# Two pieces of a spectral stage moved into the rounds of the attention before it

## The chip, the core and the metric

The kernel runs on one core of a Trainium2 chip. A core has five engines that each take their own instructions in order: PE (TensorE, matrix products, with its weight loads counted apart as PEld), DVE (VectorE), ACT (ScalarE), POOL (GpSimd) and SP (SyncE, which here only issues DMAs). They meet through semaphores. Operands lie in SBUF (128 partitions), matrix results in PSUM (eight banks of 128 x 512 float32), and the large arrays in HBM. Times are device microseconds (us) of one execution.

## The reference, cut to what is touched

Two layers of a "metaformer" on eight images of 128 channels and 32 x 32 = 1024 tokens. Only the first layer matters here: an attention, and then a spectral unit whose first step is a forward sine and cosine sum over the tokens of each image.

```python
# layer 0
x = x + _L0_conv_ref(_ln_c(x), wq, wk, wv)       # attention, 8 heads of 16
t = _to_tokens(x)
t = t + _L0_ffn_ref(_ln_t(t), sigma, phi, M_u, M_plus, M_minus, ...)
x = _from_tokens(t, x)
...
def _ln_t(v, eps=1e-5):                           # over the channels of a token
    m = jnp.mean(v, axis=-1, keepdims=True)
    s = jnp.var(v, axis=-1, keepdims=True)
    return (v - m) / jnp.sqrt(s + eps)
...
Vf   = jnp.fft.rfft(phi, n=n, axis=0)             # filters
Uf_p = jnp.fft.rfft(u, n=n, axis=1)               # forward sums of an image
```

## The kernel before, in words

**The attention** (`attention_bounded`) is one long list of steps sorted by hand. `at(round, order, step)` puts a step into a round; the list is sorted by round, then by order, and every engine gets its instructions in that sequence. There are 256 rounds, 32 to an image (`first = 32 * b`), four to a unit (a quarter of the queries and half of the heads). If `t0` is the first round of a unit, then:

- `scores` (round `t0 + r`, order 0): 16 matmuls on PE into the only bank group `s`, then the exponential on ACT into a tile `e` (L598, L603).
- `add_tiles` (order 1): POOL adds the two halves of `e` into `t` (L612).
- `sums` and `reciprocals` (round `t0 + 5`, orders 4 and 5): PE adds `t` into `z` (L619), DVE takes the reciprocal `r` (L626).
- `spread_out` (round `t0 + 6`, order 2.5): PE spreads `r` into `rb` (L633).
- `divide` (rounds `t0 + 6` to `t0 + 9`, order 3): DVE multiplies `e` by `rb` (L640).
- `values` (rounds `t0 + 8` to `t0 + 11`): PE multiplies with the values into `av` (L650).
- `take` and `results` (rounds `t0 + 11`, `t0 + 12` of every second unit): ACT takes `av` out, PE turns it, ACT copies it to `at`, POOL adds it to the tokens `xt` (L660 to L674). These are the rounds 0 modulo 8. After the last quarter SP writes the image to HBM as `x1d` (L676).

Rounds 0 modulo 4 thus hold the third `divide` of a unit, and rounds 1 modulo 4 the fourth `divide` and after it the reciprocal of the next unit.

Between these lie the preparation of the next image: `load`, two `tokens` (turn the image, copy to `xt`), the 25 pieces of a layer norm (`layer_norm_pieces`: eight pairs of statistics on DVE, L79 and L80; nine pieces with 17 small POOL instructions, L87 to L99; eight normalisations on ACT, L105), two `channels`, and eight projections `keys`, `queries`, `key_values`. All these small PE results, `z` too, use one PSUM bank ("z"), so that each waits until the one before is taken out.

For image 0 the norm is made ahead (`BoundedAttention.tokens`), but its tokens are turned a second time in round 0 to have `xt`. Image 1 has its turns in rounds 8 and 12 and its norm in rounds 9 to 19.

**The spectral stage** (`Spectral.forward`) is in program order on every engine. It loads images 1, 2 and 3 (`Head.load`, L1650), makes eight sine tables `t` (`table`: on DVE two instructions with L1711 and one with L1712, on ACT one sine, L1713), norms images 1 and 2, and then takes the images in turn: `image` (PE sums p_half, L1882; ACT copies `other`, L1888; DVE adds and subtracts into `us`, L1895; PE turns), then the norm of image b + 3, then `parts`. Of image 0 the load and the norm are already made within the attention's last rounds (`Head.pieces`, one piece a round, from L745).

Of the kernel before, what the change touches and what calls it, by code (L numbers as in the profile page):

```python
# [18 lines left out]
P = 128  # L19
# [380 lines left out]
class BoundedAttention:  # L400
# [6 lines left out]
    def __init__(self, nc, cp):  # L407
        self.nc = nc
        HG, NH = self.HG, self.NH
        self.xc = cp.tile([P, T], F32, name="xc")  # L410
        self.ht = cp.tile([P, NT, C], F32, name="ht")
        self.hk = [cp.tile([P, T], F32, name=f"hk{n}") for n in range(2)]
        self.wq = cp.tile([P, HG, NH, 32], F32, name="wq")
        self.wk = cp.tile([C, C], F32, name="wk")
        self.wv = cp.tile([C, HG, NH, HD], F32, name="wv")
        self.group = cp.tile([P, NG], F32, name="group")
        self.spread = cp.tile([P, 2, P], F32, name="spread")
# [4 lines left out]
    def tokens(self, x, ident, pool, ps):  # L422

        nc = self.nc
        nc.sync.dma_start(self.xc, x[0].rearrange("c h w -> c (h w)"))
        xv = self.xc.rearrange("c (i p two) -> c two i p", two=2, p=P)
        st = pool.tile([P, NT, 6], F32, name="f_st")
        mv = pool.tile([P, NT, 2], F32, name="f_mv")
        banks = []
        for par in range(2):  # L430
            pt = ps.tile([P, 4, P], F32, tag="x", name="p_x")
            for i in range(4):
                nc.tensor.transpose(pt[:, i, :], xv[:, par, i, :], ident)
            banks.append(pt)
            for i in range(4):
                nc.vector.bn_stats(st[:, 4 * par + i, :], pt[:, i, :])
                nc.vector.bn_aggr(mv[:, 4 * par + i, :], st[:, 4 * par + i, :])
        rs = inverse_std(nc, pool, mv[:, :, 1], 1e-6, nc.vector)
        for par in range(2):
            for i in range(4):  # L440
                n = 4 * par + i
                nc.vector.tensor_scalar(
                    self.ht[:, n, :], banks[par][:, i, :], mv[:, n, 0:1], rs[:, n : n + 1],
                    ALU.subtract, ALU.mult,
                )
            pb = ps.tile([P, 4, P], F32, tag="y", name="p_y", bufs=1)
            for i in range(4):
                nc.tensor.transpose(pb[:, i, :], self.ht[:, 4 * par + i, :], ident)
            nc.scalar.copy(
                self.keys_view(0)[:, 4 * par : 4 * par + 4, :].rearrange(  # L450
                    "c r (g m) -> c r g m", m=4
                ),
                pb.rearrange("c i p -> c (i p)").rearrange("c (g r m) -> c r g m", r=4, m=4),
            )

    def matrices(self, wqT, wkT, wvT):
        nc, HG, NH = self.nc, self.HG, self.NH
# [31 lines left out]
def attention_bounded(ctx, tc, ident, x, x1d, given, weigh, head):  # L489
# [14 lines left out]
    group, spread = given.group, given.spread  # L504
    cp = ctx.enter_context(tc.tile_pool(name="a_const", bufs=1))
    sb = ctx.enter_context(tc.tile_pool(name="a_sb", bufs=2))
    ep = ctx.enter_context(tc.tile_pool(name="a_e", bufs=11))
    sp = ctx.enter_context(tc.tile_pool(name="a_s", bufs=1, space=PSUM))
    rp = ctx.enter_context(tc.tile_pool(name="a_r", bufs=1, space=PSUM))

# [149 lines left out]
        nc.scalar.copy(qrt["o"], qrt["av"][:, 0:QU])  # L660

    def results(b, img, qc, qrt):
        if qc == 0:
            img["at"] = sb.tile([P, NT, C], F32, tag="at", name="at", bufs=1)
        po = small_bank("po")
        for i in range(2):
            nc.tensor.transpose(
                po[:, i * P : (i + 1) * P], qrt["o"][:, i * P : (i + 1) * P], ident
            )
        nc.scalar.copy(  # L670
            img["at"][:, 2 * qc : 2 * qc + 2, :].rearrange("p i c -> p (i c)"), po[:, 0 : 2 * P]
        )
        mine = [img[n][:, 2 * qc : 2 * qc + 2, :] for n in ("xt", "at")]
        nc.gpsimd.tensor_add(mine[0], mine[0], mine[1])  # L674
        if qc == QC - 1:
            nc.sync.dma_start(x1d[b], img["xt"])  # L676

# [10 lines left out]
    for b in range(B):  # L688
# [6 lines left out]
        ]  # L695
        project_at = [first + n for n in (-13, -9, -5, -1, 3, 7, 11, 15)]
        if b == 0:
            turn = {"tokens": (0, 0)}
            project_at = (-1, -1, -1, 3, 4, 7, 11, 15)
        elif b == 1:  # L700
            turn = {"load": 0, "tokens": (8, 12), "channels": (18, 20)}
            norm_at = (9, 9, 10, 10, 13, 13, 14, 14) + (14, 14, 15, 15, 15, 15, 16, 16, 16) + (
                17, 17, 17, 17, 18, 18, 19, 19)
        else:
            turn = {
                "load": first - 42, "tokens": (first - 36, first - 28),
                "channels": (first - 20, first - 12),
            }
            norm_at = [first - n for n in (35, 35, 31, 31, 27, 27, 27, 27)] + [
                first - n for n in (26, 26, 25, 25, 24, 24, 23, 23, 23)  # L710
            ] + [first - n for n in (22, 22, 21, 21, 19, 18, 15, 14)]
        if b:
# [3 lines left out]
            )  # L716
            for par in range(2):
                at(turn["channels"][par], 5.5, channels, b, par)
        for par in range(2):
            at(turn["tokens"][par], 5.5, tokens, img, par)  # L720
        for n, (step, when) in enumerate(zip(project, project_at)):
            if b == 0 and n < 3:
                at(-1, 6, weigh[n])
# [18 lines left out]
            at(t0 + 11, 5, take, qrt)  # L742
            at(t0 + 12, 6, results, b, img, qc, qrt)
    end = 4 * UNITS * B
    spread_rounds(head.pieces(), (end - 40, *range(end - 30, end)))  # L745
    with tc.manual_schedule(engines=None):
        for _, _, _, do, args in sorted(work, key=lambda w: w[:3]):
            do(*args)
# [885 lines left out]
class Head:  # L1634


    def __init__(self, nc, pool, x1d):
        self.nc, self.pool, self.x1d = nc, pool, x1d
        self.x = pool.tile([P, NT, C], F32, name="x_first")
        self.odd = pool.tile([P, LOW], F32, name="odd")  # L1640
        self.at = pool.tile([P, 4, 2], F32, name="at_token")
        nc.gpsimd.iota(self.odd, pattern=[[2, LOW]], base=1, channel_multiplier=0,
                       allow_small_or_imprecise_dtypes=True)
        nc.gpsimd.iota(self.at, pattern=[[1, 4], [4 * P, 2]], base=0, channel_multiplier=4,
                       allow_small_or_imprecise_dtypes=True)

    def load(self, dst, b):
        for h in range(2):
            for sp in range(2):
# [4 lines left out]
                    self.x1d[b, sp:P:2].rearrange("p (a i h) c -> p h a i c", a=2, h=2)[:, h],  # L1654
                )

    def pieces(self):
        return [partial(self.load, self.x, 0)] + layer_norm_pieces(
            self.nc, self.pool, lambda: self.x, lambda: self.x, 1e-5
        )  # L1660


class Spectral:
# [54 lines left out]
    def forward(self, ctx, fill, head):  # L1718
# [12 lines left out]
            used += size  # L1731
            return room[:, used - size : used]

        u = [head.x] + [one.tile([P, NT, C], F32, name=f"u{n}") for n in range(1, 4)]
        u += u

        def load(b):
# [14 lines left out]
            for _ in range(2)  # L1752
        ]
        phi = early(HT)[0 : 2 * NF]
        load(1)
        nc.sync.dma_start(phi[0:NF], self.phi_e[:, PHI_PAD : PHI_PAD + HT])
        nc.sync.dma_start(phi[NF : 2 * NF], self.phi_o[:, PHI_PAD + 1 : PHI_PAD + 1 + HT])
        load_parts(0)
        load(2)
        load_parts(1)  # L1760
        load(3)
        mus = early(NFR * TAPS * C).rearrange("d (f i e) -> d f i e", f=NFR, i=TAPS)
        for f in range(NFR):
            nc.sync.dma_start(mus[:, f], self.M_u[f].rearrange("i d e -> d i e"))
        load_parts(2)

        self.shift = one.tile([P, 1], F32, name="shift")
        nc.gpsimd.memset(self.shift, -PI)
        waves = one.tile([P, 2], F32, name="at_wave")
        nc.gpsimd.iota(waves, pattern=[[2 * P, 2]], base=1, channel_multiplier=2,  # L1770
                       allow_small_or_imprecise_dtypes=True)
        times = early(4 * QT).rearrange("p (r q) -> p r q", r=4)
        nc.gpsimd.iota(times, pattern=[[1, 4], [4, QT]], base=0, channel_multiplier=0,
                       allow_small_or_imprecise_dtypes=True)
        t = one.tile([P, 4, 2, 2, LOW], F32, name="t")
        back = early(4 * 2 * 2 * QT).rearrange("p (r i a q) -> p r i a q", r=4, i=2, a=2)
        self.lags = early(4 * 2 * 8 * NF).rearrange(
            "p (r i j a k) -> p r i j a k", r=4, i=2, j=4, a=2
# [2 lines left out]
        def norm(b):  # L1781
            return layer_norm_pieces(nc, sb, lambda: u[b], lambda: u[b], 1e-5)

        for r in (0, 2, 1, 3):
            for i in range(2):
                self.table(t[:, r, i], head.odd, head.at[:, r, i : i + 1])
        for piece in norm(1):
            piece()
        self.scales(one)
        self.filters_turned(one, phi)  # L1790
        for piece in norm(2):
            piece()

        for b in range(B):
# [4 lines left out]
            if b + 3 < B:  # L1799
                load_parts(b + 3)  # L1800
                for piece in norm(b + 3):
                    piece()
            self.parts(b, pieces[b])
            if b == 1:
                self.spectra(t)
            if b == 2:
# [317 lines left out]
def metaformer_kernel(  # L2124
# [17 lines left out]
    with ExitStack() as attention:  # L2142
        given = BoundedAttention(nc, attention.enter_context(tc.tile_pool(name="att", bufs=1)))
        with ExitStack() as part:
            gram = part.enter_context(tc.tile_pool(name="gram", bufs=1))
            gps = part.enter_context(tc.tile_pool(name="gram_ps", bufs=2, space=PSUM))
            given.tokens(x, ident, gram, gps)
            scores_are_small(nc, gram, gps, wqT, wkT, flag)
            given.matrices(wqT, wkT, wvT)
        bounded = nc.values_load(flag[0:1, 0:1], min_val=0, max_val=P)  # L2150
        with tc.If(bounded > P - 1) as branch:
            with ExitStack() as part:
                attention_bounded(part, tc, ident, x, x1d, given, weigh, head)
        with branch.Else():
            for piece in weigh:
                piece()
            with ExitStack() as part:
                attention_general(part, tc, ident, x, wqT, wkT, wvT, x1d)
            for piece in head.pieces():
                piece()  # L2160

    layer = DeformAndExperts(
# [70 lines left out]
```

## Time and profile before

| what | us |
|---|---|
| median of three runs | 1879.45 (1876.2 to 1879.82) |
| the profiled execution: its own time | 1878.91 |
| its span, first to last instruction | 1877.2 |
| attention: first to last exponential (L603) | 32.2 to 879.8 |
| attention's last HBM write issued (L676) | 901.7 |
| first `other` of image 0 (L1888) | 936.8 |
| forward sums over, PE runs on with p_g | 1037 |

Busy shares of the span are PE 89%, DVE 74%, POOL 62%, ACT 56%. The chain that ended last lies on PE for 55% of the span, on DVE for 15%, on POOL for 9%. A timeline row reads: start, duration, engine, line, operation, what it writes and reads, shapes, count; in brackets how long the engine was idle before it and what ended the idleness. Rows of neighbouring instructions of one kind are merged (x4). [...]

### The profile page before, as it was taken

What the parts mean: (1) busy time and instruction counts of PE and PEld (TensorE: products, weight loads), DVE (VectorE), ACT (ScalarE), POOL (GpSimd) and SP (SyncE); (2) the same over time, 40 slices, a digit from 0 to 9 for tenths busy, and PEclk for the clock granted to TensorE, in tenths of its full rate; (3) what the DMA queues carried; (4) which work ended last, traced back from release to release, by engine and by line L of the source; (5) the groups of instructions that cost most, each with busy time, mean ns of one, the idle gap of its engine ahead of it and who ended that gap; (6) DMA issues with size and microseconds to landing.
All of it is one profiled execution on the core that took longest, in us unless ns stands there. A gap on an engine that the chain in (4) does not pass through costs nothing.

```text
span 1877.2 us, 51680 instructions
## 1 busy us (share of the span) xinstructions
PE 1673.7 (89%) x22228; PEld 1024.7 (55%) x22228; DVE 1385.4 (74%) x2107; ACT 1052.6 (56%) x1676; POOL 1156.8 (62%) x1215
## 2 busy tenths in 40 slices
PE   5999999999999999998587899999888497888788
PEld 3545555555555555554133688888665363555555
DVE  2778787888888787888545666666158888999883
ACT  3666766666666666665324455555145655666630
POOL 3778777787778777786231345445126768888740
PEclk9999999999999999999688999999898588999989
DMA  1000000000000000000678322222568775855620
GB/s 30 13 2 24 2 2 24 2 24 2 24 2 24 2 2 24 2 13 2 143 176 226 122 62 71 58 62 60 183 194 262 229 223 152 237 176 164 206 83 20
DMA packets 157999, 156.17 MB, mean 83 GB/s; under 512 B 15424, under 2 KB 136864, under 8 KB 156352
## 3 DMA queue, kind: packets, MB, share of 16 engines
q1 hardware_dynamic: 142400, 102.41, 19.3%
q0 software_dynamic: 15360, 50.34, 8.7%
q8 instruction: 177, 2.90, 0.7%
q14 instruction: 62, 0.51, 0.1%
HBM read 96.39 MB, written 56.33 MB: 81 GB/s over the span
## 4 chain that ended last, share of the span: by engine, by line
PE 55%; DVE 15%; POOL 9%; ACT 8%; issue 8%; DMA 4%; SPq 2%; DVEq 0%; POOLq 0%; ACTq 0%
PE s L598 13%; PE av L650 9%; PE p_g L1951 6%; PE z L619 5%; PE p_z L2000 5%; ACT e L603 5%; PE rb L633 3%; PE p_out L1413 3%; DVE ga L1403 3%; POOL t L612 2%; DVE g L1310 2%; DMA g<-tab,idx 2%; PE pq L554 2%; PE p_mix L1245 1%; DVE e L640 1%
## 5 line engine op out<-in xcount | busy, mean ns | idle before, releaser
L612 POOL TENSOR_TENSOR t<-e 128x1024 f32<-128x1024 f32 x256 | 608.4, 2377 | 192.4 <-ACT e L603 190.2
L603 ACT ACTIVATE e<-s 128x2048 f32<-128x2048 f32 x256 | 481.0, 1879 | 261.5 <-PE s L598 254.3
L640 DVE TENSOR_TENSOR e<-e,rb 128x2048 f32<-128x2048 f32 x256 | 568.6, 2280 | 70.0 <-PE rb L633 68.6
L598 PE MATMUL s<-q,k 32*128 32x256 f32 x4096 | 299.0, 406 | 25.4 <-ACT e L603 21.2
L650 PE MATMUL av<-e,vt 128*32 128x256 f32 x4096 | 290.6, 392 | 2.9 <-DVE e L640 1.7
L1288 POOL DMA_INDIRECT g<-tab,idx x192 | 199.4, 1038 | 133.7 <-ACT cn_m L1508 67.5
L598 PEld LDWEIGHTS s<-q,k 32*128 32x128 f32 x4096 | 187.9, 187 | 153.1 <-ACT e L603 139.6
L1295 ACT ACTIVATE g<-g,w 128x128 f32<-128x128 f32 x604 | 186.2, 390 | 61.2 <-DMA g<-tab,idx 48.9
L1976 POOL TENSOR_SCALAR at<-uc 128x256 f32<-128x256 f32 (+2 forms) x62 | 75.3, 1216 | 174.1 <-issue 86.4
L626 DVE RECIPROCAL r<-z 128x256 f32<-128x256 f32 x64 | 112.5, 1757 | 94.1 <-PE z L619 94.1
L650 PEld LDWEIGHTS av<-e,vt 128*32 128x32 f32 x4096 | 102.0, 110 | 134.9 <-issue 82.6
L1951 PE MATMUL p_g<-v,a 32*128 32x128 f32 x4096 | 159.5, 285 | 9.4 <-ACT ga L1683 3.7
L1951 PEld LDWEIGHTS p_g<-v,a 32*128 32x128 f32 x4096 | 132.4, 187 | 38.3 <-issue 23.0
L1413 PE MATMUL p_out<-ga,ew 128*128 128x512 f32 x256 | 128.0, 646 | 16.4 <-DVE ga L1403 16.3
L619 PE MATMUL z<-t,group 128*32 128x256 f32 x2048 | 122.2, 379 | 0.0
L1685 DVE COPY gb<-p_g 128x512 f32<-128x512 f32 x128 | 82.4, 685 | 46.9 <-PE p_g L1951 46.2
L1685 DVE COPY ga<-p_g 128x512 f32<-128x512 f32 x128 | 82.4, 685 | 44.0 <-PE p_g L1951 44.0
L1683 ACT COPY gb<-p_g 128x512 f32<-128x512 f32 x128 | 68.7, 589 | 69.9 <-PE p_g L1951 69.1
L1683 ACT COPY ga<-p_g 128x512 f32<-128x512 f32 x128 | 68.7, 589 | 66.7 <-PE p_g L1951 66.7
L1403 DVE TENSOR_TENSOR ga<-p_g,tc 128x2048 f32<-128x2048 f32 x32 | 73.1, 2283 | 31.6 <-PE p_g L1394 31.6
L1413 PEld LDWEIGHTS p_out<-ga,ew 128*128 128x128 f32 x256 | 50.5, 206 | 76.4 <-issue 56.5
L619 PEld LDWEIGHTS z<-t,group 128*32 128x32 f32 x2048 | 66.4, 110 | 44.2 <-issue 0.3
(309 smaller groups left out, 2378.6 us busy)
## 6 DMA issues: line engine op xcount, KB each, us to landing
tab<-hx SPq DMA_DIRECT2D x24, 512.0 KB, 5.1
tab<-hx SPq DMA_DIRECT2D x72, 128.0 KB, 5.9
ud<-us SPq DMA_DIRECT2D x8, 1024.0 KB, 6.4
uc<-ud SPq DMA_DIRECT2D x16, 512.0 KB, 4.4
yd<-zs SPq DMA_DIRECT2D x32, 256.0 KB, 3.0
ga<-yd SPq DMA_DIRECT2D x32, 256.0 KB, 3.5
xc<-in_x SPq DMA_DIRECT2D x8, 512.0 KB
x1d<-xt SPq DMA_DIRECT2D x8, 512.0 KB, 3.8
```

What stands on the lines that cost most here:

```text
L598: nc.tensor.matmul(s[:, j, c, :], img["k"][rows, 2 * r + c, :], q[rows, qc * QU : (qc + 1) * QU], start=True, stop=True,)
L603: nc.scalar.activation(e.rearrange("p j c q -> p (j c q)"), s.rearrange("p j c q -> p (j c q)"), AF.Exp, scale=float(HD) ** -0.5,)
L612: nc.gpsimd.tensor_add(t, e[:, :, 0, :], e[:, :, 1, :])
L619: nc.tensor.matmul(un["z"][32 * j : 32 * j + 32, 0:QU], group, un["t", r][:, j, :], start=(r == 0), stop=(r == 3), skip_group_check=True,)
L640: nc.vector.tensor_tensor(e, e, un["rb"].unsqueeze(2).to_broadcast([P, NH, 2, QU]), ALU.mult)
L650: nc.tensor.matmul(qrt["av"][32 * j : 32 * j + 32, 0:QU], img["v"][:, 2 * r + c, P * hg + 32 * j : P * hg + 32 * j + 32], un["e", r][:, j, ...
L1288: nc.gpsimd.indirect_dma_start(out=t["g", i][:, tap].rearrange("p k c -> p (k c)"), out_offset=None, in_=rows, in_offset=bass.IndirectOffs ...
L1295: nc.scalar.activation(t["g", i][:, tap, k, :], t["g", i][:, tap, k, :], AF.Identity, scale=t["w"][:, i, tap, k : k + 1],)
L1413: nc.tensor.matmul(t["out"], self.ew[:, first + e, :], xg[:, e, :], start=(first + e == 0), stop=(first + e == NE - 1), skip_group_check=True,
L1683: self.nc.scalar.copy(dst, src)
L1685: self.nc.vector.tensor_copy(dst, src)
L1951: nc.tensor.matmul(banks[j][:, i * P : (i + 1) * P], self.a[rows, 4 * n + i, :], self.v[rows, ch].rearrange("p f k -> p (f k)"), start=Tru ...
```

## The change

The first image's tokens are kept from the first pass (`x0`: two ACT copies of 128 x 512), so round 0 of the attention turns nothing. One query projection and one value projection of image 0 move from rounds 3 and 4 to rounds 2 and 3. Image 1 is loaded in round -1, turned in rounds 4 and 8, normed in rounds 5 to 18, and its channels are turned in rounds 16 and 20 (before 18 and 20). The `e` tiles become 9 instead of 11; `at` is a small tile for each quarter.

In the last rounds the attention now also makes the norm of image 1 for the forward sums and the angles of all eight sine tables: sixteen pieces of two DVE instructions each, two pieces in each of the rounds 224, 228, ..., 252. The eight sines follow on ACT in round 260, after the last exponential. In `forward`, the load and norm of image 1 and the eight tables are gone; the first of the `parts` is loaded ahead of image 2, and `filters_turned` comes after the first image's parts. The spectral tables at images 5 and 6 stay as they were.

```diff
@@ BoundedAttention
+        self.x0 = cp.tile([P, NT, C], F32, name="x0")
...
+        for par in range(2):
+            self.nc.scalar.copy(self.x0[:, 4 * par : 4 * par + 4, :], banks[par])
@@ attention_bounded
-    ep = ctx.enter_context(tc.tile_pool(name="a_e", bufs=11))
+    ep = ctx.enter_context(tc.tile_pool(name="a_e", bufs=9))
...
         if b == 0:
-            turn = {"tokens": (0, 0)}
-            project_at = (-1, -1, -1, 3, 4, 7, 11, 15)
+            img["xt"] = given.x0
+            project_at = (-1, -1, -1, 2, 3, 7, 11, 15)
         elif b == 1:
-            turn = {"load": 0, "tokens": (8, 12), "channels": (18, 20)}
-            norm_at = (9, 9, 10, 10, 13, 13, 14, 14) + (14, 14, 15, 15, 15, 15, 16, 16, 16) + (
-                17, 17, 17, 17, 18, 18, 19, 19)
+            turn = {"load": -1, "tokens": (4, 8), "channels": (16, 20)}
+            norm_at = (5, 5, 5, 5, 9, 9, 9, 9) + (10, 10, 10, 11, 11, 11, 12, 12, 12) + (
+                13, 13, 14, 14, 17, 17, 18, 18)
...
     end = 4 * UNITS * B
-    spread_rounds(head.pieces(), (end - 40, *range(end - 30, end)))
+    angles, norms, waves = head.pieces()
+    for n, (load_first, norm) in enumerate(norms):
+        spread_rounds(load_first, (end - 43 + 2 * n,))
+        turn = end - 35 + 16 * n
+        spread_rounds(norm, [
+            turn + at for at in (0, 0, 4, 4, 8, 8, 8, 8, 9, 9, 10, 10, 10, 11, 11, 11, 11,
+                                 12, 12, 13, 13, 14, 14, 15, 15)
+        ])
+    spread_rounds(angles, [end - 32 + 4 * (n // 2) for n in range(16)])
+    spread_rounds(waves, 8 * (end + 4,))
@@ Head
+    def angles(self, r, i, cs):
+        nc = self.nc
+        nc.vector.tensor_scalar(
+            self.num, self.odd, self.at[:, r, i : i + 1], (3072.0, 2048.0)[cs], ALU.mult, ALU.add
+        )
+        nc.vector.tensor_scalar(
+            self.t[:, r, i, cs].bitcast(I32), self.num, 4095, None, ALU.bitwise_and
+        )
+
+    def waves(self, r, i):
+        flat = self.t[:, r, i].rearrange("p a f -> p (a f)")
+        self.nc.scalar.activation(
+            flat, flat.bitcast(I32), AF.Sin, scale=2 * PI / 4096, bias=self.shift
+        )
@@ Spectral.forward
-        load(1)
+        load_parts(0)
+        load(2)
         nc.sync.dma_start(phi[0:NF], ...)
         nc.sync.dma_start(phi[NF : 2 * NF], ...)
-        load_parts(0)
-        load(2)
         load_parts(1)
         load(3)
...
-        for r in (0, 2, 1, 3):
-            for i in range(2):
-                self.table(t[:, r, i], head.odd, head.at[:, r, i : i + 1])
-        for piece in norm(1):
-            piece()
         self.scales(one)
-        self.filters_turned(one, phi)
         for piece in norm(2):
             piece()
...
             self.parts(b, pieces[b])
+            if b == 0:
+                self.filters_turned(one, phi)
```

More of the change, by code (lines that the diff above doesn't have):

```diff
@@ L662, in results @@
     def results(b, img, qc, qrt):
-        if qc == 0:
-            img["at"] = sb.tile([P, NT, C], F32, tag="at", name="at", bufs=1)
+        added = sb.tile([P, 2, C], F32, tag="at", name="at")
         po = small_bank("po")
@@ L670, in results @@
         nc.scalar.copy(
-            img["at"][:, 2 * qc : 2 * qc + 2, :].rearrange("p i c -> p (i c)"), po[:, 0 : 2 * P]
+            added.rearrange("p i c -> p (i c)"), po[:, 0 : 2 * P]
         )
-        mine = [img[n][:, 2 * qc : 2 * qc + 2, :] for n in ("xt", "at")]
-        nc.gpsimd.tensor_add(mine[0], mine[0], mine[1])
+        mine = img["xt"][:, 2 * qc : 2 * qc + 2, :]
+        nc.gpsimd.tensor_add(mine, mine, added)
         if qc == QC - 1:
@@ L718, in attention_bounded @@
                 at(turn["channels"][par], 5.5, channels, b, par)
-        for par in range(2):
-            at(turn["tokens"][par], 5.5, tokens, img, par)
+        if b:
+            for par in range(2):
+                at(turn["tokens"][par], 5.5, tokens, img, par)
         for n, (step, when) in enumerate(zip(project, project_at)):
@@ L1638, in __init__ @@
         self.nc, self.pool, self.x1d = nc, pool, x1d
-        self.x = pool.tile([P, NT, C], F32, name="x_first")
+        self.x = [pool.tile([P, NT, C], F32, name=f"x_first{n}") for n in range(2)]
+        self.t = pool.tile([P, 4, 2, 2, LOW], F32, name="t")
+        self.num = pool.tile([P, LOW], I32, name="num")
         self.odd = pool.tile([P, LOW], F32, name="odd")
         self.at = pool.tile([P, 4, 2], F32, name="at_token")
+        self.shift = pool.tile([P, 1], F32, name="shift")
         nc.gpsimd.iota(self.odd, pattern=[[2, LOW]], base=1, channel_multiplier=0,
@@ L1645, in __init__ @@
                        allow_small_or_imprecise_dtypes=True)
+        nc.gpsimd.memset(self.shift, -PI)
     def load(self, dst, b):
@@ L1655, in load, with norm @@
                 )
-    def pieces(self):
-        return [partial(self.load, self.x, 0)] + layer_norm_pieces(
-            self.nc, self.pool, lambda: self.x, lambda: self.x, 1e-5
-        )
+    def angles(self, r, i, cs):
[11 more added lines that the diff above has]
+        )
+    def norm(self, n):
+        return [partial(self.load, self.x[n], n)], layer_norm_pieces(
+            self.nc, self.pool, lambda: self.x[n], lambda: self.x[n], 1e-5
+        )
+    def pieces(self):
+        angles = [
+            partial(self.angles, r, i, cs) for r in (0, 2, 1, 3) for i in range(2) for cs in range(2)
+        ]
+        waves = [partial(self.waves, r, i) for r in (0, 2, 1, 3) for i in range(2)]
+        return angles, [self.norm(n) for n in range(2)], waves
 class Spectral:
@@ L1732, in early @@
             return room[:, used - size : used]
-        u = [head.x] + [one.tile([P, NT, C], F32, name=f"u{n}") for n in range(1, 4)]
+        u = head.x + [one.tile([P, NT, C], F32, name=f"u{n}") for n in range(2, 4)]
         u += u
@@ L1765, in forward @@
         load_parts(2)
-        self.shift = one.tile([P, 1], F32, name="shift")
-        nc.gpsimd.memset(self.shift, -PI)
+        self.shift = head.shift
         waves = one.tile([P, 2], F32, name="at_wave")
@@ L1774, in forward @@
                        allow_small_or_imprecise_dtypes=True)
-        t = one.tile([P, 4, 2, 2, LOW], F32, name="t")
+        t = head.t
         back = early(4 * 2 * 2 * QT).rearrange("p (r i a q) -> p r i a q", r=4, i=2, a=2)
@@ L2158, in metaformer_kernel @@
                 attention_general(part, tc, ident, x, wqT, wkT, wvT, x1d)
-            for piece in head.pieces():
+            angles, norms, waves = head.pieces()
+            for piece in angles + [p for part in norms for p in part[0] + part[1]] + waves:
                 piece()
```

## The prediction, made before the changed kernel was run

> **What bounds the kernel now.** I read the page's groups, then the timeline of the attention's start, of its last five units, and of the 35 us behind it.
>
> In the last rounds (timeline of 850 to 880 us):
>
> ```profile
> 857.44 2.38 POOL L612 TENSOR_TENSOR t<-e 128x1024 f32<-128x1024 f32 x1 [0.85 <-ACT e L603]
> ...
> 859.78 0.74 POOL L674 TENSOR_TENSOR xt<-xt,at 128x256 f32<-128x256 f32 x1
> 860.61 2.36 POOL L612 TENSOR_TENSOR t<-e 128x1024 f32<-128x1024 f32 x1
> 860.89 1.76 DVE L626 RECIPROCAL r<-z 128x256 f32<-128x256 f32 x1 [0.83 <-PE z L619]
> ...
> 862.80 1.13 PE L633 MATMUL rb<-r,spread 64*128 64x256 f32 x8
> ...
> 864.05 8.88 DVE L640 TENSOR_TENSOR e<-e,rb 128x2048 f32<-128x2048 f32 x4 [1.41 <-PE rb L633]
> ...
> 870.27 2.38 POOL L612 TENSOR_TENSOR t<-e 128x1024 f32<-128x1024 f32 x1 [0.77 <-ACT e L603]
> ...
> 873.42 2.36 POOL L612 TENSOR_TENSOR t<-e 128x1024 f32<-128x1024 f32 x1 [0.76 <-ACT e L603]
> 873.69 1.76 DVE L626 RECIPROCAL r<-z 128x256 f32<-128x256 f32 x1 [0.76 <-PE z L619]
> ```
>
> A unit takes 12.8 us (reciprocal at 860.89, next at 873.69). PE, ACT and DVE are chained: DVE needs 8.88 for four divides, waits 0.8 for `z`, 1.76 for the reciprocal, 1.4 for `rb`. The reciprocal ends at 862.65 and PE's `rb` starts at 862.80: PE has reached it, so a late reciprocal stops PE, and with it scores, exponentials and POOL. DVE's free time per unit is thus 0.8 before the reciprocal, 0.15 behind it, and 1.4 while it waits for `rb`; what it does between two divides has 0.95 free and then lengthens the unit.
>
> Behind the attention (timeline of 900 to 948 us):
>
> ```profile
> 914.77 0.29 DVE L79 BATCH_NORM_STATS2 lp_st<-u 128x6 f32<-128x128 f32 x1
> ...
> 923.02 3.18 ACT L105 ACTIVATE u<-u,lp_nm,lp_y 128x128 f32<-128x128 f32 x8 [7.41 <-POOL lp_nm L99]
> ...
> 933.72 3.18 ACT L105 ACTIVATE u<-u,lp_nm,lp_y 128x128 f32<-128x128 f32 x8 [7.52 <-POOL lp_nm L99]
> 936.81 1.04 ACT L1888 COPY other<-p_half 128x512 f32<-128x512 f32 x2
> ```
>
> Image 0's `other` stands on ACT behind the norms of images 1 and 2, each a chain DVE, POOL, ACT. From then on every image waits for one more such chain (the next `other` at 951.85, the last of them at 1017.1), so an earlier first `other` moves everything behind it.
>
> **What the change costs and brings.**
>
> *Start, a gain.* Exponential 0 starts at 32.18, exponential 4 at 50.80. The 5.65 from exponential 0 to 1 hold the two turns; without them scores 1 follow exponential 0 and the step is 4.09, as the next: 1.56 less, and exponential 1 starts at 36.27. Scores 2 then run 38.2 to 40.3 and the moved projection to 42.3, where scores 3 may start: PE is unbroken for 4 us. In the trace PE went to its short durations (scores 1.15 instead of 2.09) at 52.6, after its first unbroken 3.4 us (row 49.2 to 52.6: busy 3.40). I take it at 42.4: exponential 3 at 43.5, exponential 4 at 46.7. That is 4.1 gained. The two `x0` copies (0.59 each, by the copy of L449) may stand before the first key's copy on ACT, or fall in ACT's idle 17 us before 19.33: 0 to 1.2 lost, taken 0.5. **-3.6**.
>
> *Second image's norm, a gain.* From exponential 17 (92.76) to 20 (108.82) are 16.1 us where three rounds take 9.6: 6.4 lost to POOL being late with `lp_nm`, and to the slow PE after it. New: 17 POOL instructions of 0.28 in rounds 10 to 12, where POOL has 0.8 free a round beside its 2.38; counting from exponential 10 I get `lp_nm` at +14.0, while ACT is at its first piece at +11.5; exponential 14 comes 2.1 late. In round 16 `channels` and `results` want the same PSUM bank, so PE waits for ACT's copy behind the exponential: 1.7. Four pairs of statistics (1.6) in the 1.4 gap, twice: 0.4. Sum 4.2 instead of 6.4: **-2.2** (ends -5 and +1).
>
> *Nine `e` tiles* cost nothing: the exponential of round k overwrites that of k - 9, whose `values` stand in PE's order before the scores of round k. The eight sines (0.72 each, L1713, and a table load of 1.28) go into ACT's idle 17.65 before 899.60. Eight SP loads more stand before nothing that is waiting.
>
> *Angles, the loss.* Alone, a piece costs DVE about 0.6: 0.37 for the multiply (0.335 in L1711, and its result is awaited) and about 0.25 for the mask (half of L1712's 0.43 with a fixed part). Two pieces are 1.25, against 0.95 free: 0.3 a unit, 2.4 in eight units. But POOL adds `t` at the same time, and this form waits for POOL. The change's own instruction, after the attention:
>
> ```profile
> 904.98 1.03 POOL L1773 IOTA ga<- 128x1024 f32 x1 [0.76 <-DMA x1d<-xt]
> 904.98 1.17 DVE L1711 TENSOR_SCALAR ga<-odd,at_token 128x256 int32<-128x256 f32 x1 [6.27 <-DMA x1d<-xt]
> ```
>
> It took 1.17 beside POOL's 1.03 and at least 0.335 without. And later, beside POOL additions like `t`:
>
> ```profile
> 1698.38 5.02 POOL L1301 TENSOR_TENSOR g<-g,w 128x512 f32<-128x512 f32 x5
> ...
> 1701.10 2.34 DVE L1045 TENSOR_SCALAR a_v<-a_mv 128x8 f32<-128x8 f32 x1
> 1703.47 0.17 DVE L1046 TENSOR_SCALAR a_b<-a_v 128x8 int32<-128x8 int32 x1
> ```
>
> Eight columns took 2.34 until POOL's last addition ended (1703.40), then 0.17. [...]
>
> Now the place. A pair of pieces follows the third divide, 6.66 after the divides start. In round 252 that is 870.71, inside `t` (870.27 to 872.65). The first multiply ends 0.1 after `t`; the rest needs 0.9, just inside POOL's gap up to 873.42. The pair ends at 873.65, 2.95 after it came: 2.0 over the 0.95. If the last mask misses the gap it waits for another `t`: 4.4. In rounds 0 modulo 8 (224, 232, 240, 248) POOL has `xt` behind `t` and only 0.09 free: from 857.83 the pair waits to the end of the second `t` at 863.0 and needs 1.0 more: 6.15, so 5.2 over. As `rb` gates both sides, the phases return in each unit. After 5 us without PE work its clock falls (granted clock 0.50 in the row 888.9 to 892.3, after a stretch with PE busy 1.42 of 3.4): POOL then comes later and the next pair may slip through, but PE takes about those 2 us instead. So I keep 2.0 for the other units: 4 x 5.2 + 4 x 2.0 = 28.8. Image 0's old statistics between the divides (0.4 a unit, two units) go: -0.8. **+28.0**. By the durations alone it would be +1.6; DVE's divides would hide nearly all. I take the locked value because the same form shows it beside POOL work, and POOL adds three quarters of the time; ends 1.6 and 38 (4.4 in all four lighter units).
>
> *Behind the attention, a gain.* Only image 2's norm now stands before `other`. Its first statistics wait for the load, behind 512 KB of `x1d` and 1 MB of `parts`: 2.1 MB. From 902 the windows show 266, 184, 115, 151, 254 and 185 GB/s in steps of 2 us: 1.94 MB by 912, so about 912.9. One norm is 914.77 to 926.2 = 11.4; `other` at 924.3 instead of 936.81. DVE's `scales` are done by then, and `filters_turned` (2.4 on POOL) falls where POOL waits 9.6 for the statistics. **-12.4** (ends -8, the load at 917, and -15.5, at 909.8).
>
> **Sum**: -3.6 - 2.2 + 28.0 - 12.4 = +9.8 on 1878.9, so 1888.7; the median of the runs shown is 0.5 higher: **1889**.
>
> **Rivals.**
>
> 1. *The lock doesn't bite* in this form of two inputs and output in SBUF, or the phases leave DVE in POOL's gaps: tail +1.6, the sum -3.6 - 2.2 + 1.6 - 12.4 = -16.6, 1863. For it: DVE has 0.8 idle a unit and the pieces are short. Against: the rows above. 16%.
> 2. *The lock costs half*: the load and cold PE leave DVE free passage in every second unit: tail +14, sum -4.2, 1875. The sign turns where the eight pairs lose less than 18.2 together, 2.3 a unit. 11%.
> 3. *Every instruction waits its own `t`*: where POOL wins after each DVE instruction, a pair passes four of them, some 9 us over: 8 x 9 - 0.8 = +71, sum +53, 1933. Against: POOL idles 0.8 a round and DVE then needs 0.3. 8%.
> 4. *The forward gain is hidden*: the DMAs are busy from 902 to 934 (share about 1), so image 2 lands late: gain 8 or less, sum +14, 1893; counted with the forecast.
>
> Forecast with its lock ends (about 1880 to 1900): 65%.
>
> **How the numbers follow.** The range must leave out at most 2 in 10: most of rival 3 above 1904 and the lower part of rival 1 below 1863. A measurement tells no change from 0.2%, 3.8 us. Slower: 65 less what lies below 1883.2 (6), and rival 3: 67; within: 6 of these and 3 of rival 2: 9; faster: 16 + 8 = 24. The likeliest case alone: 1880 to 1900.
>
> **What would show it.** Right: L1711's successors in the attention at a mean above 0.6 us instead of 0.35, their ends just behind the ends of `t` or `xt`; units of some 18 us at 224 to 248 and 15 between; exponential 4 near 46.7; image 0's `other` some 23 us after the last `x1d` write is issued, instead of 35. Wrong: angles of 0.3 each and units still 12.8; then rival 1 holds. If the units lengthen but `other` comes 30 us after the write, the load is the wait.

## The result and the profile after

| | before | after |
|---|---|---|
| median, us | 1879.45 (1876.2 to 1880.55, 5 runs) | 1886.48 (1885.35 to 1888.57, 5 runs) |
| ratio to before, 95% interval | | 1.0055 (1.0037 to 1.0072) |
| span of the profiled execution | 1877.2 | 1884.3 |
| exponential 4 starts | 50.80 | 46.76 |
| exponential 20 starts | 108.82 | 101.40 |
| exponential 255 starts | 877.91 | 897.13 |
| last `x1d` write issued | 901.7 | 920.3 |
| first `other` | 936.81 | 944.17 |

The changed kernel is slower by 7.0 us in the medians; the interval of the ratio is 7 to 13.5 us. The exponentials are the attention's beat, so the difference in the start of the same exponential shows where time goes. After minus before, cumulative:

```
exponential     4      20     100    226    227    231    235    239    243    247    251    255
us            -4.04  -7.42  -7.5   -7.55  -1.88  -0.51  +3.80  +5.18  +11.65 +13.04 +17.49 +19.22
```

The start gains 7.4, two hundred rounds keep it, and the last 29 exponentials lose 26.8. Behind them 11.2 come back: `other` is 7.4 late where the write was 18.6 late, and the span ends 7.1 later. (Lines of the changed kernel: `t` L616, `rb` L637, divide L644, `xt` L677, `x1d` L679, the angles L1677 and L1680, sines L1686, loads L1667, `m` L1786, `other` L1923.)

The timeline of the changed kernel over round 224 and the round 228 after it:

```profile
772.36 2.37 POOL L616 TENSOR_TENSOR t<-e 128x1024 f32<-128x1024 f32 x1 [0.81 <-ACT e L607]
772.71 2.17 DVE L1677 TENSOR_SCALAR num<-odd,at_token 128x256 int32<-128x256 f32 x1
...
774.69 0.79 POOL L677 TENSOR_TENSOR xt<-xt,at 128x256 f32<-128x256 f32 x1
774.92 0.71 DVE L1680 TENSOR_SCALAR t<-num 128x256 int32<-128x256 int32 x1
775.53 2.36 POOL L616 TENSOR_TENSOR t<-e 128x1024 f32<-128x1024 f32 x1
...
775.66 2.38 DVE L1677 TENSOR_SCALAR num<-odd,at_token 128x256 int32<-128x256 f32 x1
...
778.08 0.29 DVE L1680 TENSOR_SCALAR t<-num 128x256 int32<-128x256 int32 x1
...
782.29 1.34 PE L637 MATMUL rb<-r,spread 64*128 64x256 f32 x8 [4.50 <-DVE r L630]
...
783.57 2.09 PE L602 MATMUL s<-q,k 32*128 32x256 f32 x16
...
791.36 2.37 POOL L616 TENSOR_TENSOR t<-e 128x1024 f32<-128x1024 f32 x1 [1.21 <-ACT e L607]
791.45 2.42 DVE L1680 TENSOR_SCALAR t<-num 128x256 int32<-128x256 int32 x1
```

POOL's `t` ends at 774.73, the first multiply at 774.88; `xt` ends at 775.48, the first mask at 775.63; the second `t` ends at 777.89, the second multiply at 778.04. Three instructions of 0.3 us of work each end 0.15 us behind the POOL instruction that was under way. The two pieces together take 5.66 us (772.71 to 778.37), the reciprocal behind it is late, PE stands 4.5 us in front of `rb`, and the next scores take 2.09 instead of 1.15 at the lower clock (granted 0.57 in 783.5 to 787). In round 228 one of the four instructions meets a `t`, and takes 2.42.

The groups of the angles, with busy time and mean ns:

```profile
L1677 DVE TENSOR_SCALAR num<-odd,at_token 128x256 int32<-128x256 f32 x16 | 21.3, 1334 | 0.3
...
L1680 DVE TENSOR_SCALAR t<-num 128x256 int32<-128x256 int32 x16 | 10.5, 658 | 0.6
```

For the same multiply into `ga`, behind the attention, the mean before was 398 ns.

Behind the attention, the timeline of the changed kernel from the last `x1d` write to image 2's first statistics:

```profile
920.29 0.33 SPq L679 DMA_DIRECT2D x1d<-xt  x1
...
923.67 0.52 SPq L1786 DMA_DIRECT2D m<-in_M_plus  x1
...
924.87 2.58 SPq L1667 DMA_DIRECT2D u<-x1d  x4
...
932.87 0.29 DVE L79 BATCH_NORM_STATS2 lp_st<-u 128x6 f32<-128x128 f32 x1 [5.67 <-DMA u<-x1d]
```

Its timeline of 940 to 946 us, where image 2's one norm ends and image 0's `other` follows:

```profile
941.08 3.18 ACT L105 ACTIVATE u<-u,lp_nm,lp_y 128x128 f32<-128x128 f32 x8 [6.57 <-POOL lp_nm L99]
944.17 1.04 ACT L1923 COPY other<-p_half 128x512 f32<-128x512 f32 x2
```

One norm stands between the write and `other` instead of two. But SP issues nothing for 3.4 us behind the `x1d` write, and its waits from 900 to 940 us name the cause of 2.2 of these (waiting engine and line, what it waited for, total us, times, longest):

```profile
SPq L1786 <- DMA x1d<-xt: 2.2, 1, 2.2
```

### The profile page after: what moved, and what is told of

It reads as the page before. It is cut to its first block, busy times and chain, and to the rows that moved or that the text cites. A ratio compares the mean times of both kernels' runs of the same rounds, so it can differ in the third digit from the quotient of the medians.

```text
span 1884.3 us, 51650 instructions
## 1 busy us (share of the span) xinstructions
PE 1668.4 (89%) x22220; PEld 1024.0 (54%) x22220; DVE 1407.8 (75%) x2115; ACT 1054.6 (56%) x1678; POOL 1157.0 (61%) x1215
## 3 DMA queue, kind: packets, MB, share of 16 engines
q1 hardware_dynamic: 142400, 102.41, 19.1%
## 4 chain that ended last, share of the span: by engine, by line
PE 19%; DVE 14%; issue 5%; POOL 5%; ACT 3%; DMA 3%; SPq 2%; DVEq 0%; ACTq 0%; POOLq 0%
PE p_g L1986 6%; PE p_z L2035 5%; DVE ga L1416 3%; PE p_out L1426 2%; DVE g L1323 2%; PE p_mix L1258 1%; DVE zs L2047 1%; POOL g L1301 1%; SPq L1224 1%; DMA g<-tab,idx 1%; PE p_half L1917 1%; PE p_g L1407 1%; PE po L2151 1%; DVE sm L1324 1%; PE po L2136 1%
## 5 line engine op out<-in xcount | busy, mean ns | idle before, releaser
L616 POOL TENSOR_TENSOR t<-e 128x1024 f32<-128x1024 f32 x256 | 608.1, 2375 | 207.1 <-ACT e L607 204.9
L644 DVE TENSOR_TENSOR e<-e,rb 128x2048 f32<-128x2048 f32 x256 | 568.7, 2281 | 66.3 <-PE rb L637 66.3
L637 PE MATMUL rb<-r,spread 64*128 64x256 f32 x512 | 75.4, 414 | 22.9 <-DVE r L630 22.9
```

Source lines behind the costliest of these rows:

```text
L616: nc.gpsimd.tensor_add(t, e[:, :, 0, :], e[:, :, 1, :])
L644: nc.vector.tensor_tensor(e, e, un["rb"].unsqueeze(2).to_broadcast([P, NH, 2, QU]), ALU.mult)
```

## The experiments

The runs come from three chips; each ratio is to the kernel before on the same chip (1876.79, 1923.06 and 1879.22 us there). "Lock" in the prediction and the expectations is a name for the wait of these TENSOR_SCALARs for POOL (2.17, 0.71 and 2.38 us in round 224 for 0.3 of work); the runs show how long it lasts, not what makes it. "Tail" is how much exponential 255 minus exponential 226 grew against the kernel before; it is 26.8 in the changed kernel.

**Angles behind the attention.**

```diff
-    spread_rounds(angles, [end - 32 + 4 * (n // 2) for n in range(16)])
-    spread_rounds(waves, 8 * (end + 4,))
+    spread_rounds(angles, 16 * (end + 5,))
+    spread_rounds(waves, 8 * (end + 9,))
```

> The sixteen angle pieces come after the attention's last divide (round 261) and the sines after its last result (round 265); all else as in the changed kernel. Lock theory: the units are 12.8 us again, the last x1d write is issued 26 us earlier than in the changed kernel (near 894), and the angles fit into DVE's idle 16 us before the first statistics of image 2: the time is 1886.5 - 26 = 1860 (1856 to 1865). Rival, the second norm in the last rounds or the slower PE clock makes the loss: 1880 or more. Rival, the angles then delay image 0's first `other`: 1864 to 1870.

Measured: ratio 0.9991 (0.998 to 1.0002), 1874.48 us; 1860 had been expected. The tail is 7.1, so 19.7 of 26.8 hang on the angles. The 7.1 left are the norms': the exponentials lose at 234 (2.41), 236 (1.41), 250 (2.39) and 251 (0.92). The first two belong to image 0's norm. The kernel before made it too in its last rounds, one piece a round; the change put its pieces into rounds 221 to 236. Of the 19.1 that exponential 255 is sooner than in the changed kernel, only 12.7 reach the first `other` (931.48), for SP then waited longer for its first load of `m`, as its waits from 890 to 930 us show:

```profile
SPq L1786 <- DVE t L1680: 5.2, 1, 5.2
...
SPq L1786 <- ACT t L1686: 0.7, 1, 0.7
```

The loads now wait for the angles and the sines. What in the program ties them together is open.

**The same place on DVE, other instructions.** Each pair of angle pieces becomes four BATCH_NORM_STATS2 over 192 columns, 1.54 us for four. The tables stay zero, so this kernel leaves the forward sums out.

```diff
-        nc.vector.tensor_scalar(self.num, self.odd, self.at[:, r, i : i + 1], ...)
-        nc.vector.tensor_scalar(self.t[:, r, i, cs].bitcast(I32), self.num, 4095, None, ...)
+        for _ in range(2):
+            nc.vector.bn_stats(self.st, self.odd[:, 0:192])
```

> [...] Lock theory: no waiting for POOL, 0.4 us a unit, 1886.5 - 24 = 1863 (1859 to 1867). Rival, any work between the third and the fourth divide costs what the angles cost: 1886.

Measured in one run: 1865.18 us; tail 6.5, no more than the 7.1 of the norms without angles. The statistics of round 224:

```profile
771.77 1.54 DVE L1680 BATCH_NORM_STATS2 st_dummy<-odd 128x6 f32<-128x192 f32 x4
```

They start 0.36 behind the start of a `t` of 2.38 and do not wait for it. By the exponentials they cost 0.3 to 0.4 in four of the five units in which no norm is late and nothing in the fifth; in the three with late norms the loss is 0.3 to 1.3 smaller than without them. So more DVE work than the angles' own (1.25) in the same place costs little.

**The same instructions on 8 of 256 columns.**

```diff
-            self.num, self.odd, self.at[:, r, i : i + 1], ...
+            self.num[:, 0:8], self.odd[:, 0:8], self.at[:, r, i : i + 1], ...
-            self.t[:, r, i, cs].bitcast(I32), self.num, 4095, ...
+            self.t[:, r, i, cs, 0:8].bitcast(I32), self.num[:, 0:8], 4095, ...
```

> The angle instructions stay in their form and places but cover 8 columns instead of 256, 0.17 us each alone; the tables are otherwise zeros, so the forward sums are not computed. Lock theory: each pair still waits out POOL's t, 2 to 5 us a unit, so the time is 1876 to 1885 and these instructions reach 2 us beside t. Rival, the cost is DVE's own work: 0.7 us a pair fits into the free 0.95, 1861.

Measured in one run, which leaves the forward sums out as well: 1883.25 us; tail 20.1, so 13.6 beyond the statistics' 6.5, of the 20.3 that the full pieces cost over them. The timeline at round 224:

```profile
772.96 2.05 DVE L1678 TENSOR_SCALAR num<-odd,at_token 128x8 int32<-128x8 f32 x1
...
774.94 0.72 POOL L678 TENSOR_TENSOR xt<-xt,at 128x256 f32<-128x256 f32 x1
775.04 0.65 DVE L1682 TENSOR_SCALAR t<-num 128x8 int32<-128x8 int32 x1
...
775.99 2.22 DVE L1682 TENSOR_SCALAR t<-num 128x8 int32<-128x8 int32 x1
```

Eight columns take 2.05 and 2.22. The multiply ends at 775.01 and the masks at 775.69 and 778.21, just behind POOL's `t`, `xt` and `t` (774.98, 775.66, 778.19). The kind of instruction sets the cost far more than its size.

**Angles one round later, behind the reciprocal.**

```diff
-    spread_rounds(angles, [end - 32 + 4 * (n // 2) for n in range(16)])
+    for n, piece in enumerate(angles):
+        at(end - 31 + 4 * (n // 2), 5.9, piece)
```

> Each pair of angle pieces comes one round later, behind the reciprocal and ahead of the statistics, where DVE waits 1.4 us for rb and POOL's t is about to end. Lock theory with the phases of the trace: the first multiply waits 0.3 us, the pair passes in POOL's gap of 1.0, and at most 0.5 us a unit is lost: 1861 to 1866. Rival, POOL wins wherever the pieces stand: 1875 to 1886.

Measured: ratio 0.9951 (0.9938 to 0.9964), 1868.14 us, a little above the 1866 expected at most; tail 6.35, less than the norms' own 7.1. In sum the angles cost nothing there, though two multiplies, in rounds 233 and 249, still take 2.32 each. In round 225:

```profile
775.94 2.37 POOL L616 TENSOR_TENSOR t<-e 128x1024 f32<-128x1024 f32 x1
...
777.89 0.57 DVE L1678 TENSOR_SCALAR num<-odd,at_token 128x256 int32<-128x256 f32 x1
...
778.49 0.29 DVE L1681 TENSOR_SCALAR t<-num 128x256 int32<-128x256 int32 x1
778.82 0.35 DVE L1678 TENSOR_SCALAR num<-odd,at_token 128x256 int32<-128x256 f32 x1
779.20 0.29 DVE L1681 TENSOR_SCALAR t<-num 128x256 int32<-128x256 int32 x1
...
779.33 2.39 POOL L616 TENSOR_TENSOR t<-e 128x1024 f32<-128x1024 f32 x1 [1.03 <-ACT e L607]
```

The first multiply comes 0.4 before this `t` ends (778.31) and costs 0.57; the other three start in POOL's gap of 1.03 behind it, and DVE had to wait for `rb` (to 779.25) in any case. What is left of the tail is the norms', seen on ACT in front of exponential 234 of the same kernel:

```profile
804.78 0.88 ACT L105 ACTIVATE x_first<-x_first,lp_nm,lp_y 128x128 f32<-128x128 f32 x2 [2.62 <-POOL lp_nm L99]
```

**The norms of the tail spread out**, from 16 rounds each to 30 (rounds 169 to 198 and 201 to 230), once with the angles in their old place and once in the gap.

```diff
-        spread_rounds(load_first, (end - 43 + 2 * n,))
-        turn = end - 35 + 16 * n
-        spread_rounds(norm, [turn + at for at in (0, 0, 4, 4, 8, 8, 8, 8, 9, ...)])
+        turn = end - 87 + 32 * n
+        spread_rounds(load_first, (turn - 4,))
+        spread_rounds(norm, [turn + 4 * (k // 2) for k in range(8)] + [
+            turn + 13 + k for k in range(17)])
```

> The changed kernel with the angles in their places, but the two norms of the forward sums made earlier and thinner: statistics in pairs behind the reciprocals of rounds 169 to 181 and 201 to 213, one of the nine POOL pieces a round (182 to 190, 214 to 222), one normalisation a round. Theory from the run with the angles at the end: the norms' own loss of 7 us (ACT waiting for lp_nm at exponentials 234 to 236 and 250 to 251) goes, the angles' 20 us stays: exponential 255 about 6.5 us earlier than in the changed kernel, time 2 to 4 us above the kernel before. Rival, both losses overlap in the same units and only the larger counts: no more than 2 us below the changed kernel, which is 7 to 10 us above before.

> The angles behind the reciprocals (as in the run that placed them there) and the norms spread as above. Theory: both losses gone, exponential 255 some 7 us ahead of the kernel before, the last x1d write issued near 895, time 15 to 17 us below the kernel before. Rival, the spread pieces only move the loss to other rounds: 9 us below, as with the angles alone.

Measured with the angles in place: ratio 1.0046 (1.0025 to 1.0066), 10.4 us over the kernel before in the medians; tail 31.2: longer by 4.4, though 7.1 of the norms' loss had been taken away. The theory failed. The rival's time came out, but not its reason, for then the tail would have stayed at 26.8. By the exponentials, each heavy unit (rounds 0 modulo 8) now loses 6.3 to 6.5; in the changed kernel two of the four (232 and 248) lost only 4.4 and 4.5, and 2.45 and 2.44 of these are ACT's waits for `lp_nm` at exponentials 234 and 250. The angles' own part there was 1.9 and 2.0. In round 232 of the changed kernel:

```profile
805.79 0.34 DVE L1677 TENSOR_SCALAR num<-odd,at_token 128x256 int32<-128x256 f32 x1
805.84 0.38 POOL L94 TENSOR_SCALAR lp_w<-lp_w 128x8 f32<-128x8 f32 x1
806.17 0.29 DVE L1680 TENSOR_SCALAR t<-num 128x256 int32<-128x256 int32 x1
...
811.45 0.88 ACT L105 ACTIVATE x_first<-x_first,lp_nm,lp_y 128x128 f32<-128x128 f32 x2 [3.13 <-POOL lp_nm L99]
```

Between the norm's small POOL instructions the first multiply and mask passed in 0.34 and 0.29 (and again at 870.98 in round 248), where round 224 has 2.17 and 0.71. With the angles in the gap: ratio 0.9876 (0.9854 to 0.9898), 24.2 us under the kernel before where 15 to 17 were expected; tail -0.2. Both losses are gone.

**Image 2's load ahead of the parts**, on top of that:

```diff
-        load_parts(0)
-        load(2)
+        load(2)
+        load_parts(0)
```

> As the last, and image 2 is loaded ahead of the first 1 MB of parts. Theory, the wait ahead of image 2's statistics is its place in the DMA queue: they start 4 to 5 us sooner after the last x1d write than 12.7 us, time 19 to 22 us below the kernel before. Rival, the wait is the last x1d write's landing alone, or the parts come late for p_a: less than 2 us gained.

Measured: ratio 0.9894 (0.9871 to 0.9916), 1901.29 us against 1898.91 without it, not told apart; in the trace, first statistics 6.9 us behind the `x1d` write instead of 12.9, and `other` 18.2 behind it instead of 24.2. The last comparison below takes up the time.

**The norms of images 2 to 7**, on top of that: their last pieces and the channels one or two rounds away.

```diff
-                "channels": (first - 20, first - 12),
+                "channels": (first - 18, first - 12),
-                first - n for n in (26, 26, 25, 25, 24, 24, 23, 23, 23)
-            ] + [first - n for n in (22, 22, 21, 21, 19, 18, 15, 14)]
+                first - n for n in (26, 26, 25, 25, 24, 24, 23, 23, 22)
+            ] + [first - n for n in (21, 21, 20, 19, 17, 16, 15, 14)]
```

> As the last, and for images 2 to 7 the normalisations come one round later, one a round, and the first channels turn in round first - 18. The kernel before loses 1.4 us in each of these images where ACT waits for lp_nm (exponential 202 to 203 takes 4.6 us instead of 3.2). Theory, the same cause: 6 x 1.4 = 8 us more, 27 to 30 us below the kernel before. Rival, the step at that round is another wait: no gain.

Measured: ratio 0.9856 (0.9827 to 0.9884). Of the 8 expected in the attention, 3 came. Each image gains 1.4 at `lp_nm`, and gives back 0.4 at the next exponential and 0.5 to 0.6 three later.

**All together on a third chip.**

> The changed kernel, beside the three variants of it on one chip. Lock theory: +7 us against the kernel before, as in the first comparison (+18.6 at the attention's last write, -11.2 behind it); the eight units of the angles lose about 27 us. Rival (the loss hangs on where POOL and DVE happen to stand on one chip): another sum of the eight units than 25 to 29.

> Angles one round later behind the reciprocal, the two norms of the tail spread over 62 rounds: the tail loses below 1 us, the forward gain stays at 11: about 18 us under the kernel before, 25 under the changed one. Rival (part of the saving belongs to the slower chip on which it was seen first): 12 or less under the kernel before.

> The same with image 2's load ahead of the parts in SP's queue. Theory (SP stands with the parts behind the last x1d write's landing, and image 2 needs nothing of that write): first statistics 6 us sooner, the whole behind the attention 6 sooner, 24 under the kernel before. Rival (the load only takes its bytes from the parts, and PE waits for these later): no gain in the time over the kernel without it.

> The same, and in images 2 to 7 the norm's last pieces and its channels moved by a round or two. Seen before: 0.5 an image net, so 3 us more in the attention, 27 under the kernel before. Rival (what the images gain before round 21 they lose behind it): within 1 us of the kernel without it.

| | median, us | ratio (95% interval) | tail | last write | span |
|---|---|---|---|---|---|
| changed kernel | 1891.34 | 1.006 (1.0039 to 1.008) | 27.5 | 921.67 | 1890.4 |
| angles in the gap, norms spread | 1859.38 | 0.9904 (0.988 to 0.9929) | -0.2 | 894.23 | 1857.7 |
| and image 2's load first | 1853.35 | 0.9873 (0.9851 to 0.9895) | -0.2 | 893.43 | 1850.8 |
| and images 2 to 7 | 1850.17 | 0.9847 (0.9823 to 0.9871) | -0.2 | 889.82 | 1848.4 |

The changed kernel was 12.1 over the one before here, not 7, with the same tail as in the first comparison to 0.8. It is the same kernel: of the 6.1 by which its span is longer than in the first comparison, 1.9 lie before the first `other` and 4.3 behind it, and what made them is open. The load's 6.0 in the medians and 6.9 in the spans agree with the trace, while the two intervals overlap, and on the second chip the medians showed no gain. In the timeline of the kernel with the load first:

```profile
893.43 0.32 SPq L679 DMA_DIRECT2D x1d<-xt  x1
894.47 2.58 SPq L1667 DMA_DIRECT2D u<-x1d  x4
...
900.48 0.29 DVE L79 BATCH_NORM_STATS2 lp_st<-u 128x6 f32<-128x128 f32 x1
...
911.79 1.04 ACT L1923 COPY other<-p_half 128x512 f32<-128x512 f32 x2
```

The load leaves 1.04 behind the write and needs nothing of it, where in the kernel without this edit it left 4.64 behind it; image 2's statistics start 7.05 behind the write instead of 13.04, `other` 18.4 instead of 24.3. Of the 6.0 gained, 3.6 are the earlier issue; for the other 2.4, the statistics follow the issue by 6.0 instead of 8.4; the author puts these down to the parts' 1 MB, no longer ahead, which no run shows by itself. The last step is 3.2 in the medians and 2.4 in the spans; its intervals overlap, so it rests on the trace. There, in that kernel, the wait for `lp_nm` in front of image 7's first piece is

```profile
701.01 0.88 ACT L105 ACTIVATE ht<-xt,lp_nm,lp_y 128x128 f32<-128x128 f32 x2 [0.25 <-POOL lp_nm L99]
```

where the kernel before had 1.94. The best of the four is faster than the one before by 1.5%, and than the changed one by 2.2% (1850.17 / 1891.34).

## Why the prediction was right

It said 1889 by a sum of +9.8; the median is 1886.5, and the profiled executions differ by 7.1. The wait for POOL that it was built on was there: 14 of the 32 angle instructions began under a `t` or an `xt` and ended 0.14 to 0.16 behind it, and the other 18 took 0.29 to 0.35. That the sum came so close is in part luck, as errors in the largest term cancelled. Point by point:

| step | predicted | measured | from |
|---|---|---|---|
| start | -3.6 | -4.0 | exponential 4 |
| second image's norm | -2.2 | -3.4 | exponential 20 less exponential 4 |
| nine `e` tiles | 0 | -0.1 | exponential 226 less 20 |
| angles and the tail | +28.0 | +26.8 | exponential 255 less 226 |
| `x1d` write behind it | 0 | -0.6 | write against exponential 255 |
| behind the attention | -12.4 | -11.2 | `other` against the write |
| to the end | 0 | -0.2 | span against `other` |

*Start.* PE went to its short durations where it was put, at 42.4 (scores of 2.09 at 38.26, of 1.15 at 42.34), and exponential 4 came at 46.76 for 46.7. To be so close was luck. The prediction took this step for the end of PE's first unbroken 3.4 us, but in the trace of before PE runs unbroken from 43.85 to 47.94, 4.1 us, and its scores at 48.62 still take 2.09; the first of 1.15 come at 52.73. The granted clock reads 1.00 on both sides of the step (42.4 to 56 before, 35.6 to 45.8 after), so only the durations show it. In the traces of the experiments that start in the same way (exponential 0 at 32.14 to 32.26), exponential 3 starts at 43.60 to 44.26, for 43.59 here, and exponential 4 at 46.77 to 47.43: with the same instructions ahead of it the step comes up to 0.7 later, by the exponentials. What the profiles show is only that the last 3.4 us before the step were full (PE busy 3.40 from 49.2 to 52.6 before, 3.42 from 38.97 to 42.39 after). The `x0` copies fell in ACT's idle time before the first exponential (32.21 for 32.18), so the 0.5 for them was not lost.

*Second image's norm.* Exponential 14 came 1.6 late behind the wait for `lp_nm` (2.1 predicted) and the bank in round 17 cost 1.5 (1.7, for round 16); the old loss of 6.4 went as read, and the statistics' 0.4 did not show.

*Angles.* The wait for POOL and the place were right. Round 224 took 5.66 for a pair against 6.15, and then about one more microsecond for PE at the lower clock (scores of 2.09 for 1.15, granted 0.57). By units, heavy ones lost 6.1, 4.4, 6.5, 4.5 (5.2 predicted), the others 1.0, 1.3, 1.4, 1.7 (2.0 predicted); the pattern of heavy and light is the angles' in the first and third of the heavy ones, while more than half of the second and fourth is the norms' wait. Alone, with the norms spread out, the angles cost 31.2 for the 28.8 predicted. The statistics in the same place, at 0.3 to 0.4 a unit, and the eight columns, at two thirds of the whole cost, show that this form's wait for POOL is the cause, and the divide beside a `t` has no such wait (2.28 from 778.29, a `t` from 778.93 to 781.28); the free passage one round later shows that the place decides.

Two things under this term were wrong, and the sum fitted all the same. First, the 5.2 of a heavy unit lets the pair wait through `xt` to the end of the second `t` and then pass whole, which no run shows in the attention. In round 224 the three waiting instructions ended at 774.88, 775.63 and 778.04, each 0.15 behind another POOL instruction's end, at the next change of POOL instruction. The runs show this wait; what makes it, no run here shows. The pair came out as long because three of its four instructions each met another POOL instruction, which is rival 3's mechanism, confined to the rounds in which POOL has no gap. Second, the term held nothing for the crowded norms, which alone cost 7.1 in the tail. That the sum still fitted is due to overlap: angles alone 31.2, norms alone 7.1, both 26.8, so 11.5 of the two lie on one another or are spared by the gaps of the small POOL pieces. A prediction of 31.2 + 7.1 from the same mechanisms would have been 11.5 too high. The exponentials say where: 9.3 are missing from the angles in rounds 232 and 248, the two units with late norms, and 2.3 from the norms' second waits at 236 and 251. How much of the 9.3 is overlap and how much is gaps is open. The -0.8 for image 0's old statistics was not there either: with both losses gone the tail is -0.2.

The free time of 0.95 between two divides was a little small: the statistics' 1.54 should then have cost 0.6 in each of eight units; they cost 0.3 to 0.4 in four of the five units without late norms, and nothing in the fifth.

*Behind the attention.* The norm and the bytes in front of the load were right in kind, 12.6 from the write to the first statistics for 11.2. Missing was the wait of 2.2 that loading the parts ahead of image 2 puts in front of SP's whole queue: the parts wait for the write to land. "Eight SP loads more stand before nothing that is waiting" was said of the loads within the attention; that the parts' new place brings a wait of its own was left out. With image 2 first again, its statistics come 6.0 sooner behind the write; the time was 6.0 lower in one pair of comparisons and no lower in the other.

*Rivals.* That the lock does not bite (16.6 under the kernel before) fits the angles' new place (8.7 under it, with 6.35 of the norms' loss still in), not the old one. The half cost (1875) would need a tail of 14; the sign turned at 18.2, and the angles alone, with the norms out of the way, cost 31.2. The hidden forward gain (8 or less) did not come: 11.2 were gained.

## What to carry to other kernels

In this kernel a short TENSOR_SCALAR from SBUF to SBUF on DVE cost at least the rest of the POOL instruction that it met, with 8 columns as with 256 (2.05 and 2.22 us beside a `t` against 2.11 to 2.44; 0.29 to 0.35 where no `t` or `xt` was under way). Place such an instruction where POOL is about to be idle and where DVE waits anyway, and price it by POOL's timeline, not by its duration. Two crowded pieces of work in the same rounds need not add: here 31.2 and 7.1 made 26.8, and spreading out the norms alone lengthened the tail. When loads are reordered, ask of the first in the queue what it waits for, since all behind it wait too.

## What was not expected of the hardware

Beside back-to-back POOL instructions, three DVE instructions in a row each ended 0.15 us behind the POOL instruction under way, which is less than the 0.35 of a multiply and the 0.29 of a mask, as if they began before POOL's records end. The row of before, with five additions on POOL in a row (8 columns, 2.34 us), had shown no such turn-taking: at some 1.0 us for an addition (5.02 for five), the instruction passed over the ends of two and came behind the last. What sets the two apart is open. In the tail of the changed kernel PE's clock was at 0.57 (783.5 to 787 us) after PE had stood 4.5 us in front of `rb` (777.79 to 782.29), so that one late reciprocal cost about a microsecond more than its wait (scores of 2.09 for 1.15).
